# Attention row sums gathered by quarters of columns, one reciprocal for two heads, and a new order of the pieces

## The chip, the cores and the metric

The kernel runs on one core of a Trainium2 chip. The metric is the device time of one execution in microseconds (us); lower is better. The profile's times are counted from the start of its span.

## The reference, cut to what matters

The input is 8 images of 512 channels and 32 x 32 pixels, all in fp32. Two layers follow each other, each on a group-normalised input and with a residual:

```python
x = x + _L0_conv_ref(_gn(x), ...)   # 1x1 conv, two bottlenecks with attention, 1x1 conv
x = x + _L1_conv_ref(_gn(x), ...)   # depthwise 3x3, relu, prune, 1x1 conv, relu, prune

for i in range(N):                  # N = 2 bottlenecks
    yi = ys[-1]
    z = cbs(yi, m_cv1_w[i], m_cv1_bn[i], 1)          # 3x3 conv, norm, silu
    z = bot_attention(z, m_qkv_w[i], m_rw[i], m_rh[i])
    z = jax.nn.silu(bn_eval(conv2d(z, m_cv2_w[i], 0), m_cv2_bn[i]))
    ys.append(yi + z)

# bot_attention: 4 heads of 64 channels, 1024 tokens
logits = jnp.einsum('bhdi,bhdj->bhij', q, k + r) * HD ** (-0.5)
a = jax.nn.softmax(logits, axis=-1)
out = jnp.einsum('bhij,bhdj->bhdi', a, v)
```

The change is about the softmax's denominators: for each of the 1024 tokens i the sum over j of the exponentials, its reciprocal, and the multiplication of the 64 output rows of a head by it.

## The kernel before

One program works through the 8 images. An image passes through the pieces of layer 0 (group norm; a 1x1 convolution, `ps_cv` and `ps_y`; for each of two bottlenecks a 3x3 convolution by products in a transformed space, `ps_c`; queries and keys, `ps_qk`, and values, `ps_v`; the attention; a 1x1 convolution, `ps_m`; then a 1x1 convolution over all parts, `ps_cv2q`, `ps_cv`) and of layer 1 (group norm, 3x3 depthwise taps on VectorE, relu and prune, a 1x1 convolution, `ps_q` or `ps_pw`, relu and prune). Every piece is a small Python function. It is put with `add` (L307) into a list under a short name, and `go` (L310) reads a string of names and emits the next piece of each name. `FIRST` (L45) holds the order for the first image, `HEAD` (L64) and `TAIL` (L80) for the others, `LAST` (L87) for the end of the last image. So the order on every engine is written by hand: each of TensorE, VectorE, ScalarE and SyncE is wrapped in `InOrder` (L95), which keeps its instructions in the order in which they were emitted. GpSimd is not wrapped, but its instructions too are issued one after another. Because of the wrapper nearly all instructions have the line L105 in the profile and are told apart by their tiles' names. Only the semaphores of the real data dependences make engines wait for each other.

The names that matter here: `g gm gd gv gp gb ga` are the pieces of a group norm (L445): statistics of half a chunk on VectorE, a small matmul `pm`, means, a small matmul `pv`, `gp` (rs: an addition on VectorE and a power on GpSimd, L480), the bias nb, and the application to a chunk on ScalarE. `fo` (L260) has two pieces that fold the batch norms' constants: the first writes `sc` on VectorE and raises 24 columns to a power on GpSimd (L264), the second uses it in six small VectorE operations. `c` are the 1x1 convolution's first products (`ps_cv`), `ta`, `ti`, `to` weight transforms, `t` depthwise taps, `l lr lp` relu, maximum and prune of a chunk (for the last image the prune multiplies the chunk's weights, `wring`, on VectorE; for the others the chunk itself, on GpSimd, L615), `o O` products of the 1x1 convolution of layer 1 (`ps_q`, `ps_pw`), `q qa` query products and their end.

The attention (L971) works on pairs of heads m = 0, 1. For each pair, each half ih of the tokens i and each block jt of 128 tokens j there is one step: `s` scores (four 64x64 tiles of 512 columns), `e` the exponential on ScalarE, `p` the running sum `sum` over the steps on VectorE, `w` the product with the values (`ps_av`). After the 16 steps of a pair come:

- `n` (L1030): four matmuls with a weight of 32 columns of ones, each into its own 32 rows of a PSUM bank `ps_dn`: row group i has the sums over j for 512 tokens of one head and one half, the same in all 32 rows.
- `nr` (L1039): the reciprocal of that bank by VectorE, in four pieces of 128 columns.
- `nc`: two passes on ScalarE that sum the denominators and their reciprocals, to be compared with a limit at the end.
- `ns` (L1045): two DMAs on SyncE's queue, one for each half of the tokens, that copy the reciprocals into `rw`: 64 rows, each twice, so that each of the 64 output rows of a head has its own.
- `sc` (L1059): the multiplication of `z` by `rw`, half by half, and then `m`, the products `ps_m` that read `z`.

The banks `ps_dn` come from a pool of one buffer, which the small matmuls `pm` and `pv` share. An fp32 matmul has two passes in the profile, with a weight load each. Transfers on SyncE's queue are issued in the emitted order: input chunks, ring weights `wring`, `rw` and outputs.

Of the kernel before, what the change touches and what calls it, by code (L numbers as in the profile page):

```python
# [42 lines left out]


FIRST = """  # L45
    g*6 gm gd gv g gp g gb gm gd ga gv ga c gp fo gb c ta0 ga ta0 ga ta0 ti0 fo ta2 to0*2 c
    ti0*2 ca ta2*2 c rl ca ta1*3 ti2 ti1 to1 d ti1 d y ya to1 ti1 y ya ti2 to2 d y ti2 d to2 rl
    ya y d*2 ya d P Rc R P d*3 Rc R d*2 P Rc R B P Rc R B*2 P*2 Rc R E Ez B Rc R E Ez k*2 X k dw
    ta0 ka k kp ka ta0*2 v kp ti0 v va ti0 v ti0 q v va ta1 q ta1 qa q*2 qa ta1 s e s e p to0 s
    e p w to0 s e w*2 ti1 s e p ti1*2 p s e p w s to1 s e p w e p w s w to1 ta2 e s e w h p z  # L50
    ta2 s e p ta2 s ti2 e w*2 s e w ti2 to2 ti2 s e w s e to2 w s e w s e w s e rh p w p*5 h z
    s*2 w e*2 n s e w p s p w nr e p w nr*2 s e nc s nr e ns p w s e p w*2 nc s e p w h z s e s
    w s*2 p*2 e w p e*2 p sc p w sc s w e p w s e p w*3 h z n nr*4 ns nc sc Q K m ma sc dp mr
    m*2 ma mr m ma mr ma mr d*4 Q nc K d*3 P d P Rc R d*2 Rc R d*2 P Rc R P*2 Rc B R B P Rc R E
    Ez Rc B*2 R E Ez k X dx k*3 ka*2 kp*2 v*2 q v*2 va*2 cw*3 rk cw q*2 qa q qa s*2 e*2 p s e p
    w s e w s p cw*2 e s e w s e p rk p w s e p*2 s e w s e g*2 w*2 p w h z s e w cw s e p*2
    cw*2 rk s e w*2 s e w s*2 p e rk w p s e g w p g p s*2 e g w g e*2 p w h z p s w e g p w n
    nr s e nr p w g s e s p w nr e s e w p w*2 s nr p e s e w h ns p s e p nc*2 s w e p w s e p
    w s e p w s sc e p s e p w sc w*3 h z n nr*2 Q nr*2 ns z Q sc*2 nc m*2 ma mr ma mr m ma nc m
    ma mr gm mr gd Q gv u A Q x u i A x i gp i*2 Q gb ga*4 Q im id Q iv A Q x ip i*2 ib b bm t*3  # L60
    Q A t x i*2
"""

HEAD = """  # L64
    t c*2 t b im id bm c ca iv t ip t l t*2 ib lr b t*3 c bm ca b y d y bm d ya d*2 ya d*3 y P d
    Rc R d*2 P Rc R d ya P d Rc R B P Rc R P B*2 Rc R E P Ez Rc B R E Ez y k*3 ya k ka X lp ka
    kd*2 t*5 v*2 l t va v*2 va t lr q*2 t*2 lp t q qa s q e qa s e p s t e w t s e w l s*2 p*2 w
    e*2 p w s p e s w t s w t e s e p lr e p w*2 h z s e p w s t w s p s e p e*2 w*2 p s e w s t
    e p s w p s e w e t p*2 w lp t h z s*2 e*2 w s*2 n e p*2 e w*2 s nr s p e w nr e p s e w nr
    s nr t p ns l w e p*2 w lr lp w ot h s e s w p ot w s w s e*2 p*2 e w p s e w s e ot p*2 z  # L70
    sc w nc w*2 h n nc o O nr ok Ok z nr*2 sc nr ns o ou oa O*2 Ou sc Oa m sc nc m*2 ma*2 m ma
    mr ot mr ma mr o nc mr ou d Ou o O d ou Ou o d O ou*2 oa Ou*2 d Oa o O P d*2 Rc d*3 R P d*2
    Rc R d P Rc P R B Rc P B Rc P R B*2 Rc R ou E oa Ou R Oa o O dp E Ez*2 X k v k v ou oa Ou
    fr*2 Oa ka kd f*2 fr*2 f*2 dx va k v*2 k va q*4 ka kd qa*2 s*3 e*2 p e w p s e w s*2 e*2 p*3
    w s*2 g e*2 w*2 s p e w*2 s e w p s*2 h g e g p w s w z p e*2 s w e g*2 s*2 w*2 p e*2 g p*3
    g s w*2 e p s e w h s*2 e*2 p z p w*2 s p e p s n nr*3 w e s g e p w p s w*3 e p s nc e nr s
    ns e nc w s h s p w z w e p s e w s p e*2 p sc s w e p*2 w s sc e p w*3 h n nr*4 ns z
"""

TAIL = """  # L80
    Q*2 K r2 nc r0 Q r2 sc Q m r0 sc K m*2 ma nc mr ma m r0*2 ma mr r1*2 mr Q*3 ma mr r2 r1*2 u0
    r2 a0 u1 gm a1 gd Q x1 u0 r3 gv x0 gp r3*2 u0 Q r3 gb u0*2 Q u0 a0 i a0 ga Q i x0*2 ga Q i
    u0 a0 i im id ga Q iv ip u1 x0 Q u1*2 ib u1 b a1 x1 bm Q ga u1 t a1 i t Q x1 u1 i*2 a1 t i t
    x1
"""
# [40 lines left out]
def fast_kernel(  # L126
# [1230 lines left out]
    def check_range():  # L1357

        oks = small.tile([P, 1], F32, tag="oks", name="oks", bufs=1)

# [514 lines left out]
```

## Time and profile before

| what | value |
|---|---|
| time, median of 3 runs | 2594.34 us (2594.32 to 2595.45) |
| span of the profiled execution | 2593.6 us |
| mean granted TensorE clock | 0.997 |
| TensorE passes busy | 2557.7 us, 14806 recorded |
| VectorE busy | 2054.9 us |
| ScalarE busy | 1214.4 us |
| `ps_dn` passes, 128x32 tiles of 512 columns | 40.3 us, 605 ns each, 256 |
| reciprocals of 128 columns | 113.7 us, 925 ns each, 128 |
| `rw` DMAs, 256 KB each | 64, 523 to 1814 ns of issue, 3.1 to 4.2 us from issue to landing |

The profiled execution's span runs from its first to its last instruction; the page gives no separate time for what lies around it, so the span stands beside the median of the timed runs, 0.74 us below it. The busy time of passes counts overlapping ones once. A row of the timeline gives start, length, engine, line, operation, output tile, input tiles and shape; the bracket at the end is the engine's idle time before it and what ended it. A pass's listed length (592 ns for 512 columns) is longer than the distance to the next one's start (429 ns), since passes overlap.

### The profile page before, as it was taken

What the parts mean: (1) busy time and instruction counts of PE and PEld (TensorE: products, weight loads), DVE (VectorE), ACT (ScalarE), POOL (GpSimd) and SP (SyncE); (2) the same over time, 40 slices, a digit from 0 to 9 for tenths busy, and PEclk for the clock granted to TensorE, in tenths of its full rate; (3) what the DMA queues carried; (4) which work ended last, traced back from release to release, by engine and by line L of the source; (5) the groups of instructions that cost most, each with busy time, mean ns of one, the idle gap of its engine ahead of it and who ended that gap; (6) DMA issues with size and microseconds to landing.
All of it is one profiled execution on the core that took longest, in us unless ns stands there. A gap on an engine that the chain in (4) does not pass through costs nothing.

```text
span 2593.6 us, 36377 instructions
## 1 busy us (share of the span) xinstructions
PE 2557.7 (99%) x14806; PEld 1292.0 (50%) x14806; DVE 2054.9 (79%) x2954; ACT 1214.4 (47%) x1551; POOL 129.2 (5%) x99
## 2 busy tenths in 40 slices
PE   8999999999999999999999999999999999999997
PEld 5454463634636346463464635545355544645443
DVE  8887588877897877877778778787788877888657
ACT  3635446353463544635445444544445454363534
POOL 1000000000100000000000000000001000010000
PEclk9999999999999999999999999999999999999998
DMA  9445230522305214060140702306122151312300
GB/s 347 157 155 203 66 122 25 167 98 73 113 27 199 66 65 122 17 247 18 65 122 17 248 18 81 105 24 241 33 96 75 61 204 34 130 45 82 122 17 34
DMA packets 83791, 268.51 MB, mean 104 GB/s; under 512 B 7072, under 2 KB 37536, under 8 KB 69408
## 3 DMA queue, kind: packets, MB, share of 16 engines
q1 hardware_dynamic: 76032, 248.01, 27.2%
q0 software_dynamic: 4032, 14.68, 3.1%
q10 hardware_dynamic: 3552, 3.41, 0.4%
q8 instruction: 118, 1.93, 0.3%
q14 instruction: 57, 0.47, 0.1%
HBM read 212.34 MB, written 36.96 MB: 96 GB/s over the span
## 4 chain that ended last, share of the span: by engine, by line
PE 95%; DVE 3%; ACT 1%; issue 0%; DMA 0%; SPq 0%; DVEq 0%; ACTq 0%
PE ps_av L105 16%; PE ps_s L105 16%; PE ps_c L105 13%; PE ps_cv L105 12%; PE ps_qk L105 8%; PE ps_cv2q L105 8%; PE ps_q L105 7%; PE ps_v L105 4%; PE ps_y L105 4%; PE ps_m L105 4%; PE ps_dn L105 1%; ACT qy L105 1%; DVE sum L105 1%; DVE ht L105 1%; PE ps_pw L105 0%
## 5 line engine op out<-in xcount | busy, mean ns | idle before, releaser
L105 ACT ACTIVATE e<-ps_s 128x1024 f32<-128x1024 f32 x512 | 509.7, 1023 | 286.8 <-PE ps_s L105 265.6
L105 PE MATMUL ps_s<-qy,kr 64*64 64x512 f32 x4096 | 513.7, 592 | 1.4
L105 DVE TENSOR_TENSOR sum<-sum,e 128x1024 f32<-128x1024 f32 x384 | 475.2, 1238 | 39.2 <-ACT e L105 19.9
L105 PE MATMUL ps_av<-e,vt 64*64 64x512 f32 x4096 | 506.2, 590 | 0.0
L105 DVE SCALAR_TENSOR_TENSOR ht<-xn,v_sb,ht 128x961 f32<-128x961 f32 (+1 forms) x256 | 317.3, 1247 | 8.6 <-ACT ht L105 5.0
L105 PEld LDWEIGHTS ps_s<-qy,kr 64*64 64x64 f32 x4096 | 160.5, 132 | 289.0 <-issue 191.1
L105 PEld LDWEIGHTS ps_av<-e,vt 64*64 64x64 f32 x4096 | 165.4, 133 | 277.4 <-issue 266.0
L105 PE MATMUL ps_qk<-z,wring 128*128 128x512 f32 x512 | 231.1, 596 | 2.0 <-ACT z L105 1.3
L105 DVE TENSOR_TENSOR sum<-e 128x1024 f32<-128x1024 f32 x64 | 78.1, 1220 | 164.0 <-ACT e L105 162.6
L105 ACT COPY c<-ps_c 128x256 f32<-128x256 f32 x96 | 35.6, 371 | 259.4 <-PE ps_c L105 259.3
L105 PEld LDWEIGHTS ps_qk<-z,wring 128*128 128x128 f32 x512 | 95.6, 190 | 115.7 <-issue 101.5
L105 DVE RECIPROCAL r<-ps_dn 128x128 f32<-128x128 f32 x128 | 113.7, 925 | 11.2 <-PE ps_dn L105 9.0
L105 PE MATMUL ps_c<-vt,wring 128*128 128x128 f32 x1024 | 119.4, 276 | 2.3 <-DVE v L105 1.3
L105 PEld LDWEIGHTS ps_c<-kr,wring 128*128 128x128 f32 x1024 | 116.8, 192 | 8.0 <-issue 6.1
L105 PEld LDWEIGHTS ps_c<-vt,wring 128*128 128x128 f32 x1024 | 116.2, 192 | 4.3 <-ACT c L105 2.3
L105 PE MATMUL ps_c<-qy,wring 128*128 128x128 f32 x1024 | 117.0, 275 | 0.0
L105 PE MATMUL ps_c<-kr,wring 128*128 128x128 f32 x1024 | 117.0, 275 | 0.0
L105 PE MATMUL ps_cv<-pt,w_sb 128*128 128x512 f32 x256 | 116.7, 607 | 0.0
L105 PE MATMUL ps_v<-wring,z 128*128 128x256 f32 x512 | 115.9, 379 | 0.7 <-DVE kr L105 0.7
L105 PEld LDWEIGHTS ps_c<-qy,wring 128*128 128x128 f32 x1024 | 115.6, 192 | 0.0
L105 PE MATMUL ps_m<-z,wm_sb 128*128 128x512 f32 x256 | 112.5, 592 | 0.0
L105 PE MATMUL ps_y<-pt,w_sb 128*128 128x512 f32 x256 | 112.3, 592 | 0.0
(178 smaller groups left out, 3255.5 us busy)
## 6 DMA issues: line engine op xcount, KB each, us to landing
wring<-u SPq DMA_DIRECT2D x96, 1024.0 KB, 4.8
pt<-in_x SPq DMA_DIRECT2D x32, 512.0 KB, 9.4
rw<-r SPq DMA_DIRECT2D x64, 256.0 KB, 3.4
xt<-in_x SPq DMA_DIRECT2D x32, 512.0 KB, 7.5
out<-xt SPq DMA_DIRECT2D x32, 512.0 KB, 8.0
kr<-r POOLq DMA_DIRECT2D x28, 512.0 KB, 6.6
wring<-q SPq DMA_DIRECT2D x14, 896.0 KB, 4.6
wring<-in_wqkv SPq DMA_DIRECT2D x16, 768.0 KB, 4.4
```

Source lines behind the costliest of these rows:

```text
L105: made = method(*args, **kwargs)
```

## The change

The weight of ones gets 36 columns of which only every fourth (3, 7, ...) is one. A window of 32 columns that starts at 3 - j has its ones in columns j, j + 4, and so on. The sum of a pair is now 16 matmuls of 128 columns: for each quarter j of the 512 columns, four tiles; the four quarters accumulate into the same 128 columns of the bank. Row r of a group of 32 then holds the sums of quarter r mod 4, and 128 columns hold all. One reciprocal of 128 columns does the pair; the checks read 128 columns; eight DMAs (half ih, quarter j) take the 16 rows of a quarter, each repeated eight times, into a 128-column block of `rw`.

The four strings have new orders. In `FIRST`, all eight statistics and both pieces of `fo` come before the first `gv`. In `HEAD`, the bottleneck's query products stand together ahead of the scores, and the order behind the second sum of the first bottleneck differs. `LAST` moves the taps, the last two `l lr lp` and the products `o` against each other. Elsewhere pieces move by a few places, and `nr` stands once per pair.

The core of the lists' diff:

```diff
 FIRST = """
-    g*6 gm gd gv g gp g gb gm gd ga gv ga c gp fo gb c ta0 ga ta0 ga ta0 ti0 fo ta2 to0*2 c
...
+    g*8 gm gd fo gm gd fo gv gp ta2 gv gp gb ga ta0 ga gb c*2 ga ta0 ga ta0 ti0 to0*2 c ti0*2 ca
...
+    ip i*2 ib b bm t*3 Q A t x i*2
 """
 
 HEAD = """
     t c*2 t b im id bm c ca iv t ip t l t*2 ib lr b t*3 c bm ca b y d y bm d ya d*2 ya d*3 y P d
...
-    kd*2 t*5 v*2 l t va v*2 va t lr q*2 t*2 lp t q qa s q e qa s e p s t e w t s e w l s*2 p*2 w
-    e*2 p w s p e s w t s w t e s e p lr e p w*2 h z s e p w s t w s p s e p e*2 w*2 p s e w s t
...
-    sc w nc w*2 h n nc o O nr ok Ok z nr*2 sc nr ns o ou oa O*2 Ou sc Oa m sc nc m*2 ma*2 m ma
...
+    Rc R d*2 P Rc R d ya P d Rc R B P Rc R P B*2 Rc R E P Ez Rc B R E Ez y k*4 ka*2 kd*2 ya X lp
+    t*5 v*2 l t v*2 va*2 lr q*2 qa q*2 qa t*4 s e lp s e p s t e w t s e w l s*2 p*2 w e*2 p w s
+    p e s w t s w t e s p lr e*2 p w*2 h z s e p w s w s t p s e p e*2 w*2 p s e w s t e p s p w
...
+    p*2 w lr lp w ot h s*2 w e p ot w s w s e*2 p*2 e p s e w*2 s ot p e p nc z sc w*3 h nc n o O
+    nr ok Ok z sc ns o ou oa O sc m ma O Ou Oa sc nc m ma m*2 ma mr ot mr ma mr o nc mr ou d Ou o
...
 """
 
...
 LAST = """
-    Q sc nc*2 m ma m sc m*2 ma rg ma mr*2 ma mr*2 Q*2 A x Q i*2 im id rg iv ip ib b bm Q*2 t A x
-    i*2 Q im id t*3 iv ip t ib t Q t b Q bm t Q*2 t A t l lr x i*2 im t lp id t iv ip t A ib t b
-    bm Q t A x t*2 l lr o x i*2 o lp o*2 im t id t o*3 iv ip t*2 o ib b t*3 bm t o*4 t*2 o*4 l t
-    lr lp t*4 l lr lp o*10 oa o*2 oa fr f oa*2 fr f o*3 oa o oa fr oa f oa fr f
+    Q sc nc*2 m ma m sc m*2 ma rg ma*2 mr*3 Q mr Q rg A Q x i*2 im id Q iv ip ib b Q A x i*2 bm t
+    Q im id t*3 Q iv ip t ib t*2 b Q bm t Q*2 t A t l lr x i*2 t im id lp t iv ip t A ib t b bm Q
+    t*2 A x t l lr o x i*2 o lp o*2 im t id t o*3 iv ip t*2 o ib b t*3 bm t o t*2 l lr lp t*5 o*7
+    l o*3 lr lp o*7 oa o*2 oa fr f oa*2 fr f o*3 oa o oa fr oa f oa fr f
 """
```

The diff of the code:

```diff
@@ -238,8 +237,9 @@
 
     r_dram = [dram.tile([P, 2, HW], F32, tag=f"r{l}", name="r") for l in range(2)]
 
-    ones = const_tile([P, 32], "ones")
-    nc.gpsimd.memset(ones, 1.0)
+    ones = const_tile([P, 36], "ones")
+    nc.gpsimd.memset(ones, 0.0)
+    nc.gpsimd.memset(ones.rearrange("p (a b) -> p a b", b=4)[:, :, 3], 1.0)
 
     rng = const_tile([P, B * 2 * HEADS], "rng")
     rng_used = [0]
@@ -1030,31 +1030,37 @@
         def sums(m):
 
             dn = dns[m] = ps_mm.tile([P, 512], F32, tag="mm", name="ps_dn")
-            for i in range(4):
-                t = sm[m, i // 2]
-                nc.tensor.matmul(
-                    dn[32 * i : 32 * (i + 1), :], ones, t[:, i % 2, :], start=True, stop=True
-                )
-
-        def reciprocal(m, q):
-            if q == 0:
-                rr[m] = work_tile("r")
-            c = slice(q * 128, (q + 1) * 128)
-            nc.vector.reciprocal(rr[m][:, c], dns[m][:, c])
+            for j in range(4):
+                for i in range(4):
+                    nc.tensor.matmul(
+                        dn[32 * i : 32 * (i + 1), :P],
+                        ones[:, 3 - j : 35 - j],
+                        sm[m, i // 2][:, i % 2, j * P : (j + 1) * P],
+                        start=(j == 0),
+                        stop=(j == 3),
+                    )
+
+        def reciprocal(m):
+            rr[m] = work_tile("r")
+            nc.vector.reciprocal(rr[m][:, :P], dns[m][:, :P])
 
         def spread(m):
 
             wide = rs[m] = work_tile("rw")
             for ih in range(2):
-                twice = rr[m][half(ih), :512].unsqueeze(1).to_broadcast([HD, 2, 512])
-                nc.sync.dma_start(wide[:, ih * 512 : (ih + 1) * 512], twice)
+                for j in range(4):
+                    some = rr[m][ih * HD + j : (ih + 1) * HD : 4, :P]
+                    at = (4 * ih + j) * P
+                    nc.sync.dma_start(
+                        wide[:, at : at + P], some.unsqueeze(1).to_broadcast([HD // 4, 8, P])
+                    )
 
         def check(m, src):
 
             n = rng_used[0]
             rng_used[0] += 1
-            src = dns[m] if src == 0 else rr[m][:, :512]
-            nc.scalar.activation(rr[m][:, 512:], src, AF.Copy, accum_out=rng[:, n : n + 1])
+            src = dns[m][:, :P] if src == 0 else rr[m][:, :P]
+            nc.scalar.activation(rr[m][:, P : 2 * P], src, AF.Copy, accum_out=rng[:, n : n + 1])
 
         def scale(m, ih):
             c = slice(ih * 512, (ih + 1) * 512)
@@ -1069,7 +1075,7 @@
         add("h", *[lambda m=m, ih=ih: part(m, ih) for m, ih in both])
         add("z", *[lambda m=m, ih=ih: join(m, ih) for m, ih in both])
         add("n", *[lambda m=m: sums(m) for m in range(2)])
-        add("nr", *[lambda m=m, q=q: reciprocal(m, q) for m in range(2) for q in range(4)])
+        add("nr", *[lambda m=m: reciprocal(m) for m in range(2)])
         add("ns", *[lambda m=m: spread(m) for m in range(2)])
         add("nc", *[lambda m=m, i=i: check(m, i) for m in range(2) for i in range(2)])
         add("sc", *[lambda m=m, ih=ih: scale(m, ih) for m, ih in both])
@@ -1364,7 +1370,7 @@
 
         def decide():
             pk = ps_mm.tile([P, 512], F32, tag="mm", name="pk")
-            nc.tensor.matmul(pk[:1, :1], oks, ones[:, :1], start=True, stop=True)
+            nc.tensor.matmul(pk[:1, :1], oks, ones[:, 3:4], start=True, stop=True)
             nc.vector.tensor_scalar(flag, pk[:1, :1], P - 0.5, None, ALU.is_lt)
 
```

More of the change, by code (lines that the diff above doesn't have):

```diff
@@ L45 @@
 FIRST = """
-    g*6 gm gd gv g gp g gb gm gd ga gv ga c gp fo gb c ta0 ga ta0 ga ta0 ti0 fo ta2 to0*2 c
[L47 to L61, printed above, removed]
+    g*8 gm gd fo gm gd fo gv gp ta2 gv gp gb ga ta0 ga gb c*2 ga ta0 ga ta0 ti0 to0*2 c ti0*2 ca
+    ta2*2 c rl ca ta1*3 ti2 ti1 to1 d ti1 d y ya to1 ti1 y ya ti2 to2 d ti2 d to2 rl d*2 y ya y
@@ new lines @@
+    ya d P Rc R P d*3 Rc R d*2 P Rc R B P Rc R B*3 P*2 Rc R E Ez Rc R E Ez k*3 ka k ka kp X dw
+    ta0*3 v kp ti0 v va ti0 v ti0 v va ta1*3 q*4 qa*2 s e s e p to0 s e p w to0 s e w*2 ti1 s e p
+    ti1*2 p s e p w s to1 s e p w e p w s w to1 ta2 e s e w h p z ta2 s e p ta2 s ti2 e w*2 s e w
+    ti2 to2 ti2 s e w s e to2 w s e w s e w s e rh p w p*5 h z s*2 w e*2 n s e w p s p w nr e p w
+    s e nc s w e ns p s e p w*2 nc s e p w h z s e s w s*2 p*2 e w p e*2 p sc p sc s w*2 e p w s
+    e p w*3 h z n nr ns nc sc Q K m ma sc dp mr m*2 ma mr m ma mr ma mr d*4 Q nc K d*3 P d P Rc R
@@ new lines @@
+    d*2 Rc R d P Rc R d P*2 B*2 P Rc R Rc R E Ez B*2 Rc R E Ez X dx k*3 ka k ka kp*2 v*2 q v*2
+    va*2 cw*3 rk cw q*2 qa q qa s*2 e*2 p s e p w s e w s p cw*2 e s e w s e p rk p w s e p*2 s e
+    w s e g*2 w*2 p w h z s e w cw s p e p cw*2 rk s e w*2 s e w s*2 p e rk w p s e g w p g p s*2
+    e g w g e*2 p w h z p s w e g p w n nr s e p w g s e s p w e s e w p w*2 s p e s e w h ns p s
+    e p nc*2 s w e p w s e p w s e p s w sc e p s e p w sc w*3 h z n nr Q ns z Q sc*2 nc m*2 ma
+    mr ma mr m ma nc m ma mr gm mr gd Q gv u Q A x u i A x i gp i*2 Q gb ga*4 Q im id Q iv A Q x
@@ L65 @@
     t c*2 t b im id bm c ca iv t ip t l t*2 ib lr b t*3 c bm ca b y d y bm d ya d*2 ya d*3 y P d
-    Rc R d*2 P Rc R d ya P d Rc R B P Rc R P B*2 Rc R E P Ez Rc B R E Ez y k*3 ya k ka X lp ka
-    kd*2 t*5 v*2 l t va v*2 va t lr q*2 t*2 lp t q qa s q e qa s e p s t e w t s e w l s*2 p*2 w
-    e*2 p w s p e s w t s w t e s e p lr e p w*2 h z s e p w s t w s p s e p e*2 w*2 p s e w s t
-    e p s w p s e w e t p*2 w lp t h z s*2 e*2 w s*2 n e p*2 e w*2 s nr s p e w nr e p s e w nr
-    s nr t p ns l w e p*2 w lr lp w ot h s e s w p ot w s w s e*2 p*2 e w p s e w s e ot p*2 z
@@ L71 @@
-    sc w nc w*2 h n nc o O nr ok Ok z nr*2 sc nr ns o ou oa O*2 Ou sc Oa m sc nc m*2 ma*2 m ma
[L72 to L76, printed above, removed]
@@ L77 @@
-    ns e nc w s h s p w z w e p s e w s p e*2 p sc s w e p*2 w s sc e p w*3 h n nr*4 ns z
+    Rc R d*2 P Rc R d ya P d Rc R B P Rc R P B*2 Rc R E P Ez Rc B R E Ez y k*4 ka*2 kd*2 ya X lp
+    t*5 v*2 l t v*2 va*2 lr q*2 qa q*2 qa t*4 s e lp s e p s t e w t s e w l s*2 p*2 w e*2 p w s
+    p e s w t s w t e s p lr e*2 p w*2 h z s e p w s w s t p s e p e*2 w*2 p s e w s t e p s p w
+    s e w e t p*2 w lp t h z s*2 e*2 w s*2 e n p*2 e w*2 s nr s p e w*2 e p*2 s e s t ns l w e
+    p*2 w lr lp w ot h s*2 w e p ot w s w s e*2 p*2 e p s e w*2 s ot p e p nc z sc w*3 h nc n o O
@@ new lines @@
+    nr ok Ok z sc ns o ou oa O sc m ma O Ou Oa sc nc m ma m*2 ma mr ot mr ma mr o nc mr ou d Ou o
+    O d ou Ou o d O ou*2 oa Ou*2 d Oa o O P d*2 Rc d*3 R P d Rc R d*2 P Rc R B P Rc B R B*2 P Rc
+    P Rc R ou E oa Ou o O dp R E Ez*2 X k Oa ou v k v oa Ou fr*2 Oa ka kd f*2 fr*2 f*2 dx va k
+    v*2 k va q ka q*2 qa q qa s*3 e*2 kd p e w p s e w s*2 e*2 p*3 w s*2 g e*2 w*2 s p e w*2 s e
+    w p s*2 h g e g p w s w z p e*2 s w e g*2 s*2 w*2 p e*2 g p*3 g s w*2 e p s e w h s*2 e*2 p z
+    p w*2 s e p*2 s e p n nr s*2 g e w*2 e s p*2 nc e s ns w*3 e nc w s h s p w z w e p s e w s p
@@ L78 @@
+    e*2 p sc s w e p*2 w s sc e p w*3 h n nr ns z
 """
 TAIL = """
[L81 to L84, printed above, removed]
+    nc*2 Q*2 K r2 r0 Q r2 Q K sc m sc m*2 ma mr ma r0*2 m r0 ma mr r1 Q r1 mr Q*2 ma mr r2 r1*2
+    u0 r2 a0 u1 gm a1 gd Q x1 u0 r3 gv u0 x0 gp r3*2 Q r3 gb u0*2 a0 i*2 x0 ga*2 Q u0 a0 Q x0 Q
@@ L85 @@
+    u0 i a0 i im id ga Q iv ip u1 x0 Q u1*2 ib u1 b a1 x1 bm Q ga t u1 a1 i t Q u1 x1 i*2 a1 t x1
+    i t
 """
 LAST = """
-    Q sc nc*2 m ma m sc m*2 ma rg ma mr*2 ma mr*2 Q*2 A x Q i*2 im id rg iv ip ib b bm Q*2 t A x
-    i*2 Q im id t*3 iv ip t ib t Q t b Q bm t Q*2 t A t l lr x i*2 im t lp id t iv ip t A ib t b
-    bm Q t A x t*2 l lr o x i*2 o lp o*2 im t id t o*3 iv ip t*2 o ib b t*3 bm t o*4 t*2 o*4 l t
-    lr lp t*4 l lr lp o*10 oa o*2 oa fr f oa*2 fr f o*3 oa o oa fr oa f oa fr f
+    Q sc nc*2 m ma m sc m*2 ma rg ma*2 mr*3 Q mr Q rg A Q x i*2 im id Q iv ip ib b Q A x i*2 bm t
```

## The prediction

> **What bounds the kernel now.** I read the page first, then the waits of TensorE, then stretches of the timeline around the sums of denominators, the start and the end. Page, busy time and chain of waits:
>
> ```profile
> PE 2557.7 (99%) x14806; PEld 1292.0 (50%) x14806; DVE 2054.9 (79%) x2954; ACT 1214.4 (47%) x1551; POOL 129.2 (5%) x99
> ...
> PE 95%; DVE 3%; ACT 1%; issue 0%; DMA 0%; SPq 0%; DVEq 0%; ACTq 0%
> ```
>
> TensorE is the bound: 99% busy and 95% of the chain. The work taken from VectorE is 79% of a span in which it is not the bound, so its size is not the gain. The waits of TensorE (engine, line, releaser: total, times, longest):
>
> ```profile
> PE pm L105 <- DVE mv L105: 9.4, 2, 8.3
> PE ps_pw L105 <- DVE wring L105: 4.7, 1, 4.7
> PE pv L105 <- DVE d L105: 3.9, 4, 1.4
> ```
>
> The first is the start, the second the last image's pruned weights. All else listed sums to 5.4 us. One more stall does not count as idle. Timeline of the second sum of one image (start, length):
>
> ```profile
> 764.26 2.55 DVE L105 TENSOR_TENSOR sum<-sum,e 128x1024 f32<-128x1024 f32 x2
> ...
> 766.23 1.69 PE L105 MATMUL ps_dn<-sum,ones 128*32 128x512 f32 x8
> ...
> 766.87 0.14 PEld L105 LDWEIGHTS ps_dn<-sum,ones 128*32 128x32 f32 x4 [0.49 <-DVE sum L105]
> ```
>
> Two of the four tiles start at 766.23, the other two at 766.87, when VectorE has ended its last addition: 0.64 us late. An undisturbed sum takes 1.06 us there, this one 1.69.
>
> **The change, step by step**, against the profiled span of 2593.6 us; the median of the runs shown, 2594.34, lies 0.74 above it, and I keep that 0.74.
>
> 1. *The streaming of a sum.* 32 sums (8 images, 2 layers, 2 pairs of heads). Before, 4 matmuls of 512 columns, each two passes: two groups of four tiles, 429 ns a group, 0.86 us. After, 16 matmuls of 128 columns: eight groups. No row has a 128x32 tile at 128 columns. The nearest is ps_c (128x128 tile, 128 columns), whose starts are 111.5 ns apart. Eight times that is 0.89: +0.03 a sum, **+1.1** in all. Bounds: +0.2 (eight quarters of 429 ns, plus a few ns each), and +2 where the sum has also its first gap of 25 ns (454 before) twice more. A far bound, in which the extra instructions set the pace, is rival A.
>
> 2. *The reciprocals.* From 4 to 1 a sum: 96 fewer at 925 ns (group row, 113.7 us by 128), so VectorE's busy time falls by 89 us. That is worth what VectorE stalls TensorE for. In layer 0's second sum it does: late starts at 450.0, 766.2, 1082.4, 1398.6, 1715.1, 2031.3, 2347.5 (0.62 each, one 0.85: 4.6 us), and in the first image at 246.0 (1.08) and 270.6 (0.60). Between an image's first and second sum stand three of the removed reciprocals, 2.8 us, against a lateness of 0.64 to 1.08. I take all: **-6.3**. Bound -3, if other DVE work fills half of it. What would be late next is the exp that the last addition reads: it ends at 764.81 (763.79 and 1.02 us), so that with a free VectorE the addition ends at 766.05, before the 766.23 of the first tiles.
>
> 3. *Lists: tile modes.* In the middle images' layer 0 the list no longer puts a score product between two query products: 39 passages from 64-wide to full mode become 32, and 23 back become 16, seven pairs. A pair costs 0.37 us by the gaps beyond streaming (0.10, 0.05, 0.11, 0.11), but the score products that now start together begin like layer 1's, with a first gap longer by 0.13: 7 x 0.235 = **-1.6** (0 to -2.6).
>
> 4. *Lists: the start.* Timeline before:
>
> ```profile
> 12.14 2.37 ACT L105 ACTIVATE pt<-pt,nb,rs 128x1024 f32<-128x1024 f32 x2 [6.19 <-DVE nb L105]
> ...
> 13.82 16.34 PE L105 MATMUL ps_cv<-pt,w_sb 128*128 128x512 f32 x32
> ...
> 14.90 4.17 POOL L264 TENSOR_TENSOR sc<-sc,mhalf 128x24 f32<-128x24 f32 x1
> ```
>
> The power of 24 columns takes GpSimd 4.17 us; now it runs after the first group norm's own power (0.72 at 11.20). The new list puts both pieces of "fo" ahead of the norm's rs and nb. So VectorE ends all four chunks' statistics and the first means at about 11.7, adds into sc by 12.0; GpSimd works 12.1 to 16.3; VectorE does the six small operations that wait for it (0.16 to 0.18 each) by 17.35; only then rs, the second variance product, rs; GpSimd's power 0.72; nb at 18.4; ScalarE 1.18 for the first chunk; first real matmul at about 20.0 instead of 13.82: +6.2. VectorE's weight transforms start at 18.4 instead of 15.08, only 3.3 later, so early waits on VectorE (1.46 at 50.8, 0.8 at 66.6, 0.5 at 74.3) shrink. I take back 1.5: **+4.7** (+3 to +6.2).
>
> 5. *Lists: the end.* TensorE waits 4.74 us for the third chunk's pruned weights, and its clock then falls (granted clock 0.52 from 2566 to 2572). The new list does that pruning one tap (1.25 us) earlier: **-1.3**. Bounds 0 and -1.7: if the clock also held, the last chunk's weights, ready at 2574.1, would end the wait.
>
> 6. *The spread.* Two DMAs a sum become eight of 64 KB: 192 more on SP. Before, 0.59 us of issue each; the nearest small one (q, 128 KB, 512 B pieces) has 0.39 to 0.50 and lands after 1.8 to 2.0. So SP is held some 4.4 us a sum rather than 1.2, and later loads behind it start up to 3.3 us later; no wait of TensorE on a DMA is listed, so I cost that at 0 (else rival B). The tight place is layer 0's second sum: TensorE has four products of 1.72 us, 6.9 us, between that sum and the first ps_m (five before). Reciprocal by 1.1, four issues by 3.2 to 3.6, landing by 5.2 to 6.2, scaling 0.69: 5.9 to 6.9. It just fits: **0**. A microsecond too late costs 8 us over the images.
>
> 7. *The checks on ScalarE* shrink from 0.59 and 0.62 us; ScalarE is 47% busy and not in the way: 0.
>
> Sum: 1.1 - 6.3 - 1.6 + 4.7 - 1.3 = -3.4, so a span of 2590.2 and **2591.0 us**. With the bounds added up: 2588 to 2599.
>
> A rule that speaks against step 1: the Trainium skill, "TensorEngine Tiling (Array Packing)", Instruction Overhead, gives each matmul some 60 cycles of overhead and advises against tiling a dimension that is already small. If 24 more passes a sum cost 25 ns each, one after another, that would be 0.6 us x 32 = 19 us, an estimate from that page, and the time about 2609. The trace has the four tiles' passes starting 6.8 ns apart (898.429, .435, .442, .449), which speaks against paying it one after another.
>
> **Rivals.**
>
> A. *The instructions of the sums set their pace* (slower). A sum now has 32 weight loads and 32 passes in 0.87 us, 73 instructions per us; what the trace shows sustained is ps_c's two per 111.5 ns, 18 per us. Fed at that pace throughout, a sum takes 32 x 111.5 = 3.57 us, +2.7 each, +87 in all; if about half are already queued, some +0.8 each, +26. It decides once four tiles' loads and passes need more than 107 ns. Against it: TensorE's sequencer passes 16 pairs within 0.18 us at 52.22 (between two of its own semaphore instructions), and pm's two passes start 28 ns apart, by which 32 would take 0.9. Also weights might not load under so short a pass: 107 more for each of 8 groups is +0.85 a sum, +27. Time 2615 to 2678, say 2618.
>
> B. *The spread comes late* (about no change to slower). The eighth DMA, or a load behind it on SP, is waited for: DVE z already waits 17.4 us in total for rw, 20 times. One us too late in 7 images is +7 to +8, with the second layer too +14: 2598 to 2606.
>
> C. *The start's loss is mostly absorbed.* With the early waits gone (2.8) and the first image's late sums eating more, it costs +2, and steps 1, 3 and 5 reach their better bounds: 2593.6 + 2 - 6.3 - 2.6 + 0.2 - 1.7 = 2585.2, so 2586.
>
> D. *The change doesn't take effect* because the late sums wait for exp, not for VectorE's throughput: step 2 at -1, 2596. It lies within the forecast's bounds and is counted there.
>
> **How the numbers follow.** Forecast 2591.0 (own range 2588 to 2599): 0.53. B 0.17, A 0.15, C 0.15. The range takes in C, the forecast and B, from 2584 to 2612, and leaves out A. About 0.2% (5.2 us) is what a measurement of this kernel can tell from no change: faster is below 2589.1, slower above 2599.5. Faster: C 0.15 and 0.12 of the forecast's lower end, 0.27. Slower: A 0.15 and 0.10 of B, 0.25. Same: 0.48.
>
> **What would show it.** RECIPROCAL x32 at about 0.93 us and DVE's busy time near 1966. ps_dn with 1024 passes whose groups start 107 to 112 ns apart, the sums 1.1 us long and none with a late half: step 1 and 2 right; groups 200 ns or more apart: A. The first ps_cv at 19.5 to 20.2: step 4; at 14 to 15: wrong. A wait of about 3.5 us for wring at the end: step 5. A wait of ps_m on DVE z released by rw, seven or fourteen times: B. Forecast wrong as a whole if new waits of TensorE in the middle images sum to more than 3 us.

## The result and the profile after

The changed kernel takes 2598.27 us (median of 21 runs, 2596.95 to 2599.94); the kernel before, on the same chip, 2594.98 (21 runs, 2593.66 to 2597.51). The ratio is 1.0014 with an interval of 1.0007 to 1.0020: 3.3 us slower, where 3.4 us faster was forecast. The profiled execution of the changed kernel has a span of 2596.0 us, 2.4 above before's, at the same clock (0.998).

The page of the kernel after: engines and chain of waits.

```profile
PE 2552.2 (98%) x15574; PEld 1314.5 (51%) x15574; DVE 1978.2 (76%) x2858; ACT 1192.2 (46%) x1551; POOL 123.7 (5%) x100
...
PE 87%; DVE 7%; ACT 3%; issue 2%; DMA 1%; POOL 0%; SPq 0%; ACTq 0%; DVEq 0%; POOLq 0%
```

VectorE is relieved by 76.7 of the 89 us foreseen, and TensorE itself is busy 5.5 us less. The span grew all the same, so TensorE waits 8 us more. Its waits in the kernel after (engine, what waits, releaser: total, times, longest):

```profile
PE pm L104 <- DVE mv L104: 7.9, 1, 7.9
PE pv L104 <- DVE rs L104: 4.7, 1, 4.7
PE ps_pw L104 <- DVE wring L104: 4.1, 2, 3.2
PE ps_dn L104 <- DVE sum L104: 3.6, 8, 0.5
PE ps_qk L104 <- ACT z L104: 2.3, 2, 2.0
```

Two of these rows are new. pv waits 4.7 us for rs: that is the start. ps_dn waits for sum eight times: those are the late sums, which should have gone. (The kernel before has late sums too, without such a row. That the row is there is not itself the loss: e13 below, the kernel before with short passes, has it as well, 3.0 us in 9, and takes no longer than before. What counts is how long the sums take.) The wait for wring at the end is shorter, as forecast.

Where the difference builds up is read by setting the same steps of the two timelines side by side (us from the start of the span):

| step of TensorE | before | after | difference |
|---|---|---|---|
| first ps_cv | 13.82 | 19.17 | +5.4 |
| first ps_qk | 67.49 | 74.34 | +6.9 |
| first sum | 121.63 | 129.58 | +8.0 |
| second image's first ps_cv | 322.94 | 330.28 | +7.3 |
| eighth image's first ps_cv | 2220.4 | 2225.5 | +5.1 |
| last ps_pw starts | 2582.25 | 2584.56 | +2.3 |
| end of the span | 2593.6 | 2596.0 | +2.4 |

The opening and what follows up to the first sum lose 8, each middle image gives 0.37 back on average (the period, from one image's first ps_cv to the next one's, is 315.83 after 316.21 in the median), the last image 2.8. So two questions were open: why the middle images give back so little, and why the start's loss grew on its way to the first sum.

### The profile page after: what moved, and what is told of

It is laid out like the page before. It is cut to its first block, busy times and chain, and to the rows that moved or that the text cites. A ratio compares the mean times of both kernels' runs of the same rounds, so it can differ in the third digit from the quotient of the medians.

```text
span 2596.0 us, 38169 instructions
## 1 busy us (share of the span) xinstructions
PE 2552.2 (98%) x15574; PEld 1314.5 (51%) x15574; DVE 1978.2 (76%) x2858; ACT 1192.2 (46%) x1551; POOL 123.7 (5%) x100
## 4 chain that ended last, share of the span: by engine, by line
PE 87%; DVE 7%; ACT 3%; issue 2%; DMA 1%; POOL 0%; SPq 0%; ACTq 0%; DVEq 0%; POOLq 0%
PE ps_s L104 14%; PE ps_av L104 14%; PE ps_c L104 12%; PE ps_cv L104 11%; PE ps_qk L104 8%; PE ps_cv2q L104 8%; PE ps_q L104 6%; PE ps_v L104 4%; PE ps_m L104 4%; PE ps_y L104 4%; DVE sum L104 2%; DVE ht L104 1%; PE ps_dn L104 1%; ACT e L104 1%; ACT qy L104 1%
## 5 line engine op out<-in xcount | busy, mean ns | idle before, releaser
L104 PEld LDWEIGHTS ps_v<-wring,z 128*128 128x128 f32 x512 | 97.1, 190 | 27.8 <-issue 12.0
```

What stands on the lines that cost most here:

```text
L104: made = method(*args, **kwargs)
```

## The experiments

**Theory.** The loss is made by the lists: the opening, and a new order in HEAD that keeps layer 0's second sums late though the reciprocals are gone. The code alone is a gain. **Rival.** The code costs: sixteen short passes, or eight DMAs, take something that the lists do not show. Where an expectation writes T3 to T5, three explanations of a slow transfer in the first image are meant, told below. Each run stands beside runs of the kernel before on the same chip. Single runs of one kernel mostly lie within 1.5 us of their median, those of the worst, e3, reach 3.4 above it, so differences under 1 us between medians are not read.

| run | what it has | median us | less before | ratio, 95% |
|---|---|---|---|---|
| after | code and lists | 2598.27 | +3.3 | 1.0014 [1.0007, 1.0020] |
| e1 | code, lists of before | 2599.74 | +4.6 | 1.0017 [1.0008, 1.0026] |
| e2 | lists, code of before | 2606.46 | +11.3 | 1.0043 [1.0030, 1.0057] |
| e3 | after, old opening | 2595.88 | +0.7 | 1.0006 [0.9997, 1.0015] |
| e4 | after, ot earlier in HEAD | 2594.12 | -1.0 | 0.9996 [0.9987, 1.0005] |
| e8 | after, score products apart | 2593.13 | -1.9 | 0.9992 [0.9983, 1.0001] |
| e6 | after, whole old FIRST | 2593.49 | -1.6 | 0.9994 [0.9985, 1.0003] |
| e5 | e6 and e4 | 2587.76 | -7.3 | 0.9970 [0.9958, 0.9982] |
| e7 | e1, one stretch of the new HEAD | 2594.52 | -0.5 | 1.0000 [0.9991, 1.0009] |
| e9 | after, ones 64 columns wide | 2599.30 | +4.1 | 1.0015 [1.0006, 1.0024] |
| e10 | e6, e8 and e9 | 2587.76 | -7.4 | 0.9973 [0.9963, 0.9983] |
| e12 | before, eight DMAs | 2595.28 | -0.4 | 0.9998 [0.9988, 1.0007] |
| e13 | before, sixteen passes of 128 | 2595.64 | 0.0 | 1.0000 [0.9991, 1.0010] |
| e14 | before, ones 36 columns wide | 2598.25 | +3.0 | 1.0011 [1.0002, 1.0021] |
| e15 | e10, tiles at their old places | 2584.35 | -10.9 | 0.9956 [0.9943, 0.9970] |
| e16 | after, tiles at their old places | 2597.26 | +2.3 | 1.0008 [0.9999, 1.0017] |
| e17 | e1, tiles at their old places | 2596.02 | +1.1 | 1.0005 [0.9996, 1.0014] |

### Code or lists: e1 and e2

e1 has the new code and all lists of before; of each four "nr" it keeps the first. e2 is the reverse: the new lists, in which every "nr" stands four times, and the old code.

```
e1:  lists of before, ... nr ...              with the sums, reciprocal, spread of after
e2:  lists of after,  ... nr*4 ...            with the sums, reciprocal, spread of before
```

> The new sums, reciprocal, spread and checks with the order of before (of every four reciprocal pieces the first place is kept). Theory T1 (the late second sum of the bottleneck's first layer is set by the exp that VectorE's first addition of the last half waits for, and by the eight additions and three subtractions pt<-ht packed behind it; removed reciprocals only make VectorE idle before that exp): the second sum of layer 0 stays late by 0.4 to 0.6 us in each middle image, VectorE shows an idle of about 2 us before the addition, sums cost 15 ns more each, first ps_cv at 13.8: time within 1.5 us of before. Rival R1 (the prediction's step 2: VectorE's backlog of reciprocals made the sums late, and the new order brings the lateness back): late sums gone, 5 to 6 us faster than before. Rival R2 (the eight DMAs or the 16 matmuls cost elsewhere): 2 us or more slower than before.

> The new order with the old sums, reciprocals (all four pieces where the one now stands), spread and checks. T1: nearly all of the change's effect is the order: first ps_cv at 19.2, first image 7 us later, then 0.3 to 0.5 us less per image and 2 us less at the end: 2 to 4 us slower than before, like the changed kernel. R2 (the new code costs): 2 us or more faster than the changed kernel. If three more reciprocals do fill VectorE ahead of the late sum (R1), 3 us or more slower than the changed kernel.

A sum's time is counted here and below from the first pass of the last four ahead of it to the first pass behind it (the prediction's 1.06 and 1.69 us are its own passes alone). e1: in the middle images layer 0's second sums take 1.60 us instead of 2.16 in the kernel before and 2.38 after. With the new matmuls alone (e13) they take 2.18, with eight DMAs alone (e12) 2.17. So the removed reciprocals, with the shorter checks at most, do end the lateness, in the order of before. That part of the prediction is right of the code. But e1 is no gain, and this has causes of its own: TensorE's waits in e1 hold a row that neither kernel has.

```profile
PE ps_m L103 <- ACT m L103: 3.4, 7, 0.5
```

Seven times, once in each middle image. ScalarE's timeline there, e1 first and then the kernel before:

```profile
1093.79 0.20 ACT L103 ACTIVATION_READ_ACCUMULATOR r<-ps_dn 128x1 f32 x1
...
1095.62 1.28 ACT L103 ACT_TABLE_LOAD   x1 [1.62 <-issue]
...
1096.91 1.45 ACT L103 ACTIVATE m<-ps_m,bi,sc 128x512 f32<-128x512 f32 x2
```

```profile
1093.18 0.20 ACT L105 ACTIVATION_READ_ACCUMULATOR r<-ps_dn 128x1 f32 x1
1093.40 1.28 ACT L105 ACT_TABLE_LOAD   x1
1094.70 0.78 ACT L105 ACTIVATE m<-ps_m,bi,sc 128x512 f32<-128x512 f32 x1
```

The table load (for m's function, silu) follows the check at once before; in e1 ScalarE idles 1.62 us and loads the table only when the first ps_m is complete (1095.55), and m comes late. The programs that are built from the two kernels show why. In e1, and in e17 below, m in each of the seven middle images takes over the buffer of the tile r that the eight DMAs of layer 0's first sum had read. It must wait for the semaphores of all eight, and five instructions that only wait stand ahead of the table load, the last of them for ps_m too. The eight transfers had landed by 1069.9; it is the wait for ps_m among them that holds up the load. In the programs of before, after, e7 and e12 no such wait stands ahead of this load.

e2 is the slowest of all: with four reciprocals in a row (3.39 us on VectorE) scores and values stall between layer 0's two sums, which lie 23.69 us apart instead of 22.63 in the kernel after, the second sum takes 2.86 us (0.36 of it is a part of that stall), and the middle image takes 316.99 in the median. Code and lists are therefore not two terms to be added (+4.6 and +11.3 give +3.3 together): the new lists need the new code.

### The table load: e7

e7 is e1, with the stretch of HEAD around and behind layer 0's second sum nearly in the new order, in which m comes earlier (and one check ahead of the sum).

```
-... z sc w nc w*2 h n nc o O nr ok Ok z sc ns o ou oa O*2 Ou sc Oa m sc nc m*2 ma*2 m ma mr ...
+... z sc w nc w*2 h nc n o O nr ok Ok z sc ns o ou oa O sc m ma O Ou Oa sc nc m ma m*2 ma mr ...
```

> The new code in the order of before, except the pieces right behind the second sum of the bottleneck's first layer, which stand as in the changed HEAD. The run with the old order throughout had in each of 7 images a wait of ps_m for ScalarE (0.65 us): the table load for silu came 1.6 us after ScalarE was free, behind a wait. T2: in the new order there the table load is done before ps_m's result is needed, that wait is gone, and the time falls by 4 to 5 us, to about 2595, as before. Rival (the wait came from the later landing of the eight DMAs): no gain, or a wait of ps_m on z instead.

The row of ps_m is gone, the load stands in time (1091.84, with m at 1093.69), and the middle image's period falls from 316.46 to 315.7. The median falls by 5.2 us against e1, as 7 x 0.76 = 5.3 has it. The late table load is what made e1 lose in the middle images; the row's 3.4 us is the part of it that the trace shows as a wait (0.5 us an image, where the expectation writes 0.65). The rest of e1's loss is a shift of the tiles, told further below (e17). The rival that the expectation names, a later landing of the DMAs, falls.

### Why the sums stay late in the changed kernel: e4 and e8

Timeline of the kernel after, TensorE, in the fourth image's layer 0 before the second sum (at 1088.9):

```profile
1072.45 1.90 PE L104 MATMUL ps_s<-qy,kr 64*64 64x512 f32 x16
1074.17 2.75 PE L104 MATMUL ps_av<-e,vt 64*64 64x512 f32 x24
...
1088.87 0.41 PE L104 MATMUL ps_dn<-sum,ones 128*32 128x128 f32 x4
1089.71 1.07 PE L104 MATMUL ps_dn<-sum,ones 128*32 128x128 f32 x28 [0.43 <-DVE sum L104]
```

ScalarE and VectorE in the same stretch:

```profile
1073.56 1.02 ACT L104 ACTIVATE e<-ps_s 128x1024 f32<-128x1024 f32 x1 [1.50 <-PE ps_s L104]
1074.48 1.23 ACT L104 ACTIVATE ht<-ht,bi,sc 128x1024 f32<-128x1024 f32 x1
1075.61 1.01 ACT L104 ACTIVATE e<-ps_s 128x1024 f32<-128x1024 f32 x1
...
1086.43 1.02 ACT L104 ACTIVATE e<-ps_s 128x1024 f32<-128x1024 f32 x1 [1.49 <-PE ps_s L104]
```

```profile
1073.45 1.22 DVE L104 TENSOR_TENSOR sum<-sum,e 128x1024 f32<-128x1024 f32 x1
1076.65 1.23 DVE L104 TENSOR_TENSOR sum<-e 128x1024 f32<-128x1024 f32 x1 [1.98 <-ACT e L104]
...
1085.98 1.22 DVE L104 TENSOR_TENSOR pt<-ht 128x1024 f32<-128x1024 f32 x1
1087.11 2.54 DVE L104 TENSOR_TENSOR sum<-sum,e 128x1024 f32<-128x1024 f32 x2
```

VectorE, the engine that was made freer, stands idle for 1.98 us at 1074.7, waiting for an exp. From there to the sum it has seven additions and three subtractions (pt<-ht, `ot` in the list, for layer 1's 1x1 convolution), of 1.2 us each but for one addition of 1.95, and hardly a gap. The exp is late because ScalarE waited 1.50 us for a score, then did one exp and a relu (ht) ahead of the next one. And the score is late because the new list issues the two score products together at 1072.45 (16 instructions), behind two products of ps_av, where the old list has them apart. The last addition ends at 1089.65, 0.78 us after the sum begins. Its own exp was there at 1087.45: it is the first addition's exp that is late, and the chain behind it has no slack.

Two edits of this stretch, in the changed kernel, should mend it: e8 puts one ps_av product back between the two scores; e4 leaves the scores together and moves the first of the subtractions (ot) in front.

```
e8  -... nr s p e w*2 e p*2 s e s t ns l w e ...
    +... nr s p e w e p*2 s e w s t ns l w e ...
e4  -... s e s t ns l w e p*2 w lr lp w ot h s*2 w ...
    +... s e s t ns l w e p ot p w lr lp w h s*2 w ...
```

> The changed kernel with one word of HEAD moved: one value product w goes between the two score products that stand together ahead of the last half of the bottleneck's first attention, so that scores and values alternate there as they did before. Theory T2 (from the runs so far: the pair of scores ends its first half one product, 0.86 us, later; its exp, the relu queued behind it on ScalarE and the next exp all follow 0.86 us later, and so does VectorE's first addition, whose chain up to the sum has no slack): the first addition starts 13.1 us ahead of the sum instead of 12.2, the second sums shrink from 2.38 to about 1.6 us, 5 to 6 us faster than the changed kernel. Rival (the subtractions packed behind it are the cause, the place of the scores is not): less than 1.5 us faster.

> The changed kernel with the first subtraction pt<-ht of HEAD moved up by five places, ahead of VectorE's first addition of the last half, into the 2 us in which VectorE waits for an exp. T1: the second sum of layer 0 is no longer late in the 7 later images (0.83 us each): 5 to 6 us faster than the changed kernel. If the lateness came from the exps themselves (ScalarE or TensorE too slow in that stretch, rival D of the prediction): less than 1 us faster.

e8: the score comes one product earlier, and VectorE begins its additions sooner. TensorE and then VectorE:

```profile
1070.27 1.04 PE L104 MATMUL ps_s<-qy,kr 64*64 64x512 f32 x8
1071.13 1.04 PE L104 MATMUL ps_av<-e,vt 64*64 64x512 f32 x8
1071.98 1.04 PE L104 MATMUL ps_s<-qy,kr 64*64 64x512 f32 x8
...
1087.55 1.13 PE L104 MATMUL ps_dn<-sum,ones 128*32 128x128 f32 x32
```

```profile
1074.47 1.23 DVE L104 TENSOR_TENSOR sum<-e 128x1024 f32<-128x1024 f32 x1 [1.12 <-ACT e L104]
```

The first addition starts 13.08 us before the sum (12.22 in the kernel after) and the sum stands in one piece: 1.60 us instead of 2.38. The median is 5.1 us below the changed kernel, against 7 x 0.78 = 5.5. e4 reaches 1.655 and 4.2 us. In both, the row "ps_dn from sum" falls from eight times (3.6 us) to one (1.0 and 1.1, in the first image). The cause is shown from both ends: the exp that starts earlier, and the VectorE work that stands behind it.

### The start: e3, e6 and e5

e3 takes the opening of FIRST (up to the first "rl") from before, e6 all of FIRST (with one nr for four), e5 the latter with e4's HEAD.

```
-g*8 gm gd fo gm gd fo gv gp ta2 gv gp gb ga ta0 ga gb c*2 ga ta0 ga ta0 ti0 to0*2 c ...
+g*6 gm gd gv g gp g gb gm gd ga gv ga c gp fo gb c ta0 ga ta0 ga ta0 ti0 fo ta2 to0*2 c ...
```

> The changed kernel with the opening of FIRST as before, up to the first ring load; nothing else. T1: first ps_cv back at 13.8; the whole lag of the first image (7.4 us at the second image's start) goes: 6 to 7.5 us faster than the changed kernel, 3 to 4 us faster than before. Rival R3 (only the 5.4 us of the first matmul are due to the opening, and the 2 us that the lag grows by later are due to other moves in FIRST): 4.5 to 5.5 us faster than the changed kernel, with 2 us of lag left at the second image.

> The changed kernel with FIRST as before (one reciprocal for four); HEAD, TAIL, LAST as changed. T2: the first image costs 6.3 us less than in the changed kernel: 2591 to 2593 us. Against the run that undid only the opening of FIRST (2.4 us less) it says what the later moves in FIRST cost; if they cost nothing, it is no faster than that run.

> The new code, FIRST as before (one reciprocal for four), HEAD, TAIL and LAST as changed, with the first subtraction pt<-ht moved up. T2: the first image's lag falls from 7.3 us to the 1.0 us that the new code with the old order showed, the late sums are gone, the end keeps its gain: 2587 to 2589 us, about 7 us faster than before. Rival (the gains do not add, since VectorE or a DMA becomes late in their place): slower than 2591.

The opening of the changed kernel works as the prediction had it. Its timeline:

```profile
11.61 4.19 POOL L264 TENSOR_TENSOR sc<-sc,mhalf 128x24 f32<-128x24 f32 x1 [6.63 <-DVE gm L104]
...
15.83 0.18 DVE L104 TENSOR_TENSOR sc<-sc,v_sb 128x24 f32<-128x24 f32 x1 [3.70 <-POOL sc L264]
...
16.92 0.58 PE L104 MATMUL pv<-d,g_sb 128*128 128x2 f32 x2 [4.73 <-DVE rs L104]
16.94 2.06 POOL L480 TENSOR_TENSOR rs<-rs,mhalf 128x2 f32<-128x2 f32 x2 [1.15 <-DVE rs L104]
```

VectorE waits 3.70 us for GpSimd's power, TensorE 4.73 us for the rs that is queued behind it on VectorE. With the old opening (e3) the first ps_cv is at 13.5 again, but the median falls by 2.4 us only, less than either reading of its expectation, and 4.9 us of lag are left at the second image: e3 loses 4.0 of it at a wait of ps_c for the weights (a DMA into wring, see below), and the later edits of FIRST stay in, as a wait of ps_qk for z shows (2.0, before 0.7). With all of FIRST (e6) the second image begins at 327.1 instead of 330.3. Together with the mended HEAD (e5) the gains add: -7.3 against before, where e6 alone has -1.6 and e4 alone -1.0, and the changed kernel +3.3: 4.9 and 4.3 make 9.2, measured 10.6.

### What is left in the first image: e9, e10, e12, e13, e14

Even with the old FIRST the second image began 4 us later than before (327.1 against 322.9), and ps_c waited for a DMA into wring. The transformed weights are written to DRAM (u) and read back into wring; the writes ran at some 340 GB/s where the kernel before has 384. T3: the new tile ones has 36 columns, not 32, and shifts all tiles behind it; 64 columns should mend that. T4: the code of the sums, the DMAs or the passes, disturbs the transfers. T5: what counts is the place of the tiles to a multiple of 256 bytes, which 64 columns do not restore either (the expectations of e9 and e14 have the sizes of the shift wrong; they stand below).

```
e9   after:   ones = const_tile([P, 64], "ones")[:, :36]
e10  e6 + e8 + the line of e9
e12  before:  eight nc.sync.dma_start a sum, each of 128 columns
e13  before:  sixteen nc.tensor.matmul a sum, each of 128 columns, ones unchanged
e14  before:  ones = const_tile([P, 36], "ones")[:, :32]
```

> The changed kernel with the tile of ones 64 columns wide instead of 36 (only the first 36 are written and used), so that all tiles behind it start at a multiple of 256 bytes again instead of 16 bytes off. In the profiles of all kernels with the 36 columns, the writes of the transformed weights (u<-uplane, u<-ucomp) between 20 and 46 us run at 340 to 345 GB/s; with the 32 columns of before at 382 to 384. Theory T3 (the shifted start of the source tiles slows these DMAs): 380 GB/s or more in that stretch, the waits of ps_c for wring and the lag behind them shrink, 0.5 to 2 us faster than the changed kernel. Rival (the new code's other parts slow them, or the placing in DRAM): 340 to 345 GB/s and no gain.

> All that the runs point to: new sums, reciprocal and spread; FIRST as before (one reciprocal for four); HEAD as changed with the one value product between the two score products; TAIL and LAST as changed; ones 64 columns wide. If the gains add: 2584 to 2587 us, 8 to 11 us faster than before; if T3 is wrong, 2586 to 2588, like the run with the old FIRST and the subtraction moved up.

> The kernel before with each of its two spread DMAs cut into four by columns (eight DMAs of 64 KB a sum, 256 in all, as in the changed kernel); nothing else. It prices the eight DMAs alone, and asks why the writes of the transformed weights between 20 and 46 us run at 340 to 345 GB/s in all kernels with the new code and at 382 to 384 in the two with the old code. Theory T4 (the number of DMAs of the program, by where or how they are kept): 340 to 345 GB/s here, the first image 1 us later. Rival (the 16 matmuls, 768 more matmul and weight load records, or something else of the new code): 382 to 384. In both the middle images stay as they are, or ps_m waits for the later landing, since the reciprocal still takes 3.7 us: up to 1 us an image; so 2595 to 2603.

> The kernel before with each sum's four matmuls of 512 columns cut into sixteen of 128, into the same places; nothing else. It prices the streaming alone: 15 ns a sum more by the changed kernel's trace (rival A of the prediction would be 0.8 us or more a sum). T4: writes between 20 and 46 us at 382 to 384 GB/s; its rival: 340 to 345. Time within 1 us of before, or 1 us more if the writes are slow.

> The kernel before with the tile of ones 36 columns wide, of which the first 32 are used as before; nothing else, so that only the places of the tiles behind it in SBUF move, by 16 bytes. Theory T5 (any move of the source tiles slows the writes of the transformed weights; the width of 64 moved them too, by 128 bytes): 340 to 345 GB/s between 20 and 46 us, ps_c's second product at 53.5 or later instead of 52.3, 0 to 2 us slower than before. Rival (the place of the tiles has nothing to do with it, the smaller reciprocal, check or the order of the memsets has): 382 to 384 GB/s.

T3 fell as it stood: with 64 columns the rate is still 342 GB/s, in e9 and e10. T4 fell: with eight DMAs (e12) or sixteen passes (e13) in the kernel before, the rate stays 383 GB/s and the time the same. T5 held: four unused columns in the kernel before, and nothing else, cost 3.0 us (0.5 to 5.5 by the interval; up to 2 were expected). The stretch from 2 to 62 us, in 40 slices of 1.5 us: GB/s, and below it the read of the weights (KB each, median us to landing); first the kernel before, then e14:

```profile
GB/s 268 392 404 412 448 408 427 410 422 414 418 422 430 139 0 358 384 384 294 273 415 268 388 285 382 322 386 384 384 374 266 416 406 407 433 440 208 410 367 338
...
wring<-u SPq DMA_DIRECT2D x6, 1024.0 KB, 6.5
```

```profile
GB/s 266 405 414 426 421 419 434 406 418 422 406 434 414 111 75 339 339 342 303 284 377 289 395 346 363 363 350 344 339 342 309 328 367 404 437 426 426 426 418 257
...
wring<-u SPq DMA_DIRECT2D x6, 1024.0 KB, 9.2
```

The loads up to slice 13 are equally fast; the writes behind it reach 384 before and 339 to 344 in e14. The reads of what they wrote, queued behind them, land after 9.2 us instead of 6.5, and e14 has a wait that the profile of before lacks: ps_c for the DMA into wring, 4.5 us. (Runs with unshifted tiles can have it too, at 1.5 to 2.5 us: e12, e13, e15, e17.) In the kernel before, the tiles from which these writes read stand at multiples of 1024 bytes within a partition, so of 256 too; 36 columns take 16 bytes more and move them by 32, 64 columns by 128 (by the addresses of the built programs). No run has a shift by another multiple of 256, so that 256 is the step that counts is not shown.

The Trainium skill, "DMA: Bandwidth & Descriptors", section "How a descriptor splits into AXI transactions", says that a transaction starts at a 256-byte boundary, so that a piece that begins behind one also pays for the bytes ahead of it. By that a piece of 1 KB needs 33 beats instead of 32 at a shift of 32 bytes (0.97 of the rate) and 36 at 128 (0.89), an estimate from that page. Measured is 0.89 in both cases (340 and 342 by 384): the direction agrees, the size only for the larger shift.

### All mended: e15, e16 and e17

The pattern of ones moves into the pool of small tiles, and an unused tile keeps its old place: e15 is e10 with that, e16 the changed kernel, e17 e1.

```
-    ones = const_tile([P, 36], "ones")
+    const_tile([P, 32], "space")
+    ones = small.tile([P, 36], F32, tag="ones", name="ones", bufs=1)
```

> The kernel with all the corrections (old FIRST, the value product between the scores), but with the pattern of ones in the pool of small tiles and an unused tile of 32 columns in its old place, so that all other tiles lie where they lay before the change. T5: 380 GB/s or more between 20 and 46 us, the wait of ps_c for wring (3.7 us) falls to 2.5 or less, 1 to 2 us faster than the run with all corrections: 2585 to 2587 us. Rival: 340 to 345 GB/s and no gain.

> The changed kernel with the pattern of ones in the pool of small tiles and an unused tile of 32 columns in its old place: all other tiles lie where they lay before the change, 256-byte aligned, and nothing else differs. It prices the shift of the tiles in the changed kernel itself. T5: 382 to 384 GB/s in the writes of the transformed weights, 0.5 to 2.5 us faster than the changed kernel (2596 to 2598 us); what is left above that against before is the order. If the changed kernel's late opening hides the slower writes: within 0.5 us of it.

> The new code in the order of before, with the tiles where they lay before. It is the new sums, reciprocal, spread and checks alone, without the shift. T5: the first image's lag of 1 us goes, the wait of ps_m for ScalarE's table load (0.65 us in 7 images) stays and the late sums stay away: 2595 to 2597 us, about as before; 2 to 4 us faster than with the shift.

The rate is back at 383 to 384 GB/s in all three. It is worth 3.4 us in e15 (against e10) and some 3.5 in e17 (+1.1 instead of +4.6), but only 1.0 in e16: in the changed kernel the late opening hides most of it (its ps_c waits 0.8 us for wring, with the old opening, in e3, 4.0). e15 takes 2584.35 us, ratio 0.9956 [0.9943, 0.9970]: 10.9 us below the kernel before and the best version here. Its waits of TensorE at the start of the list:

```profile
PE pm L104 <- DVE mv L104: 9.0, 2, 7.9
PE pv L104 <- DVE d L104: 3.5, 3, 1.5
PE ps_pw L104 <- DVE wring L104: 3.2, 1, 3.2
PE ps_c L104 <- DMA wring<-u: 1.5, 1, 1.5
```

The wait of pv for rs and the late sums of the middle images are gone (one of 1.0 us is left, in the first image); the end's shorter wait stays.

## Why the prediction was wrong

| step | forecast | measured in the traces | from |
|---|---|---|---|
| 1 streaming | +1.1 | +0.5 | 32 x 15 ns (1.535 to 1.550 us an undisturbed sum) |
| 2 reciprocals | -6.3 | +0.75 | all sums 55.96 to 57.20 us, less step 1 |
| 3 tile modes | -1.6 | -2.5 | 7 x 0.36 (scores, values, query and ps_q products of a middle image) |
| 4 start | +4.7 | +7.7 | lag at the second image, 7.3, and the 0.4 that the first image's sums gained, which step 2 counts |
| 5 end | -1.3 | about -2 | waits 4.74 to 3.19 and 0.88; the last 32 passes of ps_pw from 16.22 to 15.14 us beside that, at a granted clock of 0.90 instead of 0.82 |
| not foreseen | 0 | -2.0 | a ps_c group shorter by 0.28 in each middle image (7.66 to 7.38 us); why was not followed |

The column of measured terms sums to some +2.4, against +2.4 of the span. The span is 5.8 us above the forecast of 2590.2, step 2 alone is 7 us off. That the other misses nearly cancel (the start 3.0 dearer than forecast, the rest 4.2 cheaper) is chance.

**Step 2 failed**, in "I take all: -6.3". Its reason held for the old list (e1: 1.60 us, no late half), and most of its size in the middle images: 7 x 0.56 = 3.9 of the 4.6 taken; of the 1.7 taken in the first image e1's trace shows 0.2. But the step took the exps' times from the trace of before and asked for the last addition's alone ("so that with a free VectorE the addition ends at 766.05"). In the changed kernel that one is in time (1087.45, the sum at 1088.87). What the new list moves is the exp of the first addition of the same half: with two scores together VectorE begins this half 0.86 us later than with them apart, it idles 1.98 us, and what the reciprocals freed is lost in that gap, since the ten operations from there on fill VectorE up to the sum: 2.38 us a sum instead of 2.16. e8, which parts the scores and changes nothing else, brings 1.60. The prediction costed the list by its mode changes (step 3) and the code by its reciprocals (step 2), each with the rest as before. Even its bound of -3 was on the wrong side of what came. (The bounds of the steps, added up, give 2587 to 2599.5, not 2588 to 2599; 2598.27 lies near their upper end.) Rival D came closest: the late sums of the changed kernel do go back to an exp. But it meant those of before, which did not, as e1 shows.

**Step 4 failed in its last clause**, "I take back 1.5". The opening itself came as worked out (+5.4 at the first ps_cv, +6.2 forecast; GpSimd from 11.61 for 4.19 us). The lag then grew, by 2.6 to the first sum. The shrinking waits on VectorE were outweighed by a new one for ScalarE (ps_qk for z, +1.3) and by slower weight writes, which e16 prices at 1.0 in this kernel; some 0.3 of the 2.6 stay open. That four columns of a constant move every tile behind it was not seen at all.

**Steps 1, 3 and 5 were right** in sign, 1 smaller and 3 and 5 larger than said. Step 1: the groups of a sum, first to last pass, take 808 ns, no group waits; e13 has the same 1.550 us without any change of time. That refutes rival A and the estimate of 0.6 us a sum weighed against step 1. **Step 6 was right** for this order: no ps_m waits for rw's scaling. VectorE waits 40.0 us in 20 for rw (17.4 before), TensorE's matmuls none of it; e12 carries eight DMAs at no cost. That refutes rival B. **Step 7** was right (a check takes 0.28 us); the late table load of e1 comes from the reused buffer, not from the check. Rival C assumed that the start is absorbed; it grew.

The test that the prediction had named, "none with a late half", is the one that the profile after fails: eight sums have one. Another sign it had named, new waits of TensorE in the middle images of more than 3 us together, was just reached: 3.0 in the seven of these eight. Left open: why a shift of 32 bytes costs as much as one of 128.

## What to carry to other kernels

When a change relieves an engine and reorders the work too, follow the new order to the operand that the relieved engine waits for next, since a free engine in front of a late operand gives nothing. A list made for one version of the code is part of that version: here the new lists cost 3.3 us with the new code and 11.3 with the old. A tile that takes over another's buffer takes over its waits, so look at what stands behind them. And after any change of a constant's size, compare the DMA rates of a stretch that was not touched.

## What the runs showed of the hardware

- DMA writes to DRAM in pieces of 1 KB, out of tiles that stand 32 or 128 bytes past a multiple of 1024, ran at 340 to 342 GB/s, and at 384 at a multiple (e14, e9, e15). Loads into tiles that were shifted in the same way ran no slower (slices 2 to 13 of the two stretches shown, 392 to 448 and 405 to 434 GB/s).
- A table load of ScalarE (1.28 us) came 1.62 us after ScalarE was free in e1, where instructions that wait stand ahead of it in the program, and directly behind the check in the kernel before, where none does. e7, in which it is in time, is 0.76 us an image shorter.
- A sum of sixteen fp32 matmuls of 128 columns on 128x32 tiles (32 passes) took 1.550 us by the measure above, one of four matmuls of 512 columns (8 passes) 1.535 (e13 and before).
- GpSimd's power took 4.19 us for 24 columns, and 0.72 for two (the first group norm of the kernel before).
